# The multiply that makes LN2's shift moves from VectorE to GpSimd, and the planner's due times are set anew

## The chip, the cores and the metric

The kernel runs on one core of a Trainium2 chip. The time is the device time of one execution in microseconds; the kernel before took 4276.48 us, the median of three runs (4270.45 to 4277.21). The execution that was profiled has a span of 4280.8 us.

## The reference

One block of an image transformer, on 16 images of 128 channels x 96 x 96 pixels in float32:

```
xn1 = LN1(x)                         # over the 128 channels of a pixel
x   = x + attention(xn1)             # 8 heads, channel by channel: softmax of a 16 x 16 matrix per head
xn2 = LN2(x)                         # (x - mean) / sqrt(var + 1e-5) * w + b
h1  = w_in  x xn2                    # 128 -> 512 channels
h2  = depthwise 3x3 of h1            # nine taps for each of the 512 channels
x   = x + w_out x gelu(h2)           # 512 -> 128 channels
```

The change touches the step inside LN2 that makes, for every pixel, the numbers `rstd = (var + eps)^-0.5` and `nb = -mean * rstd`, with which the pixel's channels are scaled and shifted: `z = rstd * x + nb`.

## The kernel before

**Tiling.** An image has 24 units of 4 rows (384 pixels) and 8 bands of 12 rows (1152 pixels). The norms work on batches of 4 x 128 pixels; an image has 18, so LN1 has 288 batches in all and LN2 as many. For a batch, TensorE transposes the pixels to the partitions (`forth`, L572), VectorE takes two `bn_stats` (`stats`, L579), GpSimd makes `var/C + eps` (`variance`, L586) and raises it to -0.5 (`power`, L590). For LN2 VectorE then makes `nb` (`shift`, L594). ScalarE scales and shifts the transposed pixels (`scaled`, L621 for LN2, L617 for LN1), TensorE transposes back (`back`, L662), and ScalarE copies the result into the padded image (`place`, L666 and L668). In the first batches of the first image VectorE takes half of the scaling (L604 and L608).

**The feed-forward part.** The 512 hidden channels are four chunks of 128. For three of them, and in every second band for the fourth too, a conv job makes h1 with TensorE (`hidden`, L845), copies it to SBUF with ScalarE (`kept`, L850), and adds up nine taps: the first product is made by ScalarE (L861), two or three further products too, and those are added by accumulating DMAs that GpSimd issues (`add_products`, L869); the remaining five or six are multiply-adds of 128 x 1152 on VectorE (`tap`, L865). ScalarE ends the job with a gelu (L873). In the other bands the fourth chunk is nine matmuls per unit (L916) with a gelu of its own (L922). `ffn_out` multiplies by w_out (L939), and VectorE adds the result to x (L946). GpSimd also issues the accumulating DMAs that bring x in for LN2 (`add_x`, L542).

**What sets the order.** The program's order is written out by a planner (`Plan`) before anything runs. Each piece of work is put in with an engine, an assumed cost, and a due time: the place in the row of conv jobs, plus the offset that the table `AT` has for its kind. The planner plays the engines forward in time: an engine that is free takes, of the work whose inputs are there and whose buffers are free, the one with the earliest due time. The start times give one order, and the instructions are written in it. On the chip every engine then runs its own instructions strictly in that order, and semaphores hold an instruction until its inputs are there. So an instruction that waits holds up all that stands behind it on its engine. The tiles `st`, `ve`, `rstd` and `nb` come from a pool with four buffers for each (`small`), and the planner lets four batches be under way.

Of the kernel before, what the change touches and what calls it, by code (L numbers as in the profile page):

```python
# [9 lines left out]
F32 = mybir.dt.float32  # L10
AF = mybir.ActivationFunctionType
ALU = mybir.AluOpType
# [15 lines left out]
QT, QB = 4, 1  # L28
# [1 line left out]
X1_BUFS, XB_BUFS, PR_BUFS, H3_BUFS, ZT_BUFS = 2, 6, 5, 10, 3  # L30
IN_TURN = ("tr", "h3", "pr", "xb", "x1")
AT = dict(
    weights=5.95, zeros=1.3, load_a=-24.9, forth_a=-15.4, stats_a=-14.45, variance_a=-16.5, power_a=0.1,
    scaled_a=-8.2, gram=-10.45, back_a=-24.05, place_a=-20.25, attention=-20, mix=-9.75, residual=-0.2,
    mixed=-5.2, add_x=13.3, forth_b=-13.25, stats_b=-9.65, variance_b=-14, power_b=-10.85, shift_b=-26,
    scaled_b=4.45, back_b=-25.35, place_b=4.85, halo=7.55, hidden=0.1, kept=-2.95, product=-12.5,
    products=4.8, add_last=-15, tap=3.1, add_first=31.85, gelu=-8.35, conv=-0.05, conv_gelu=-13.5,
    out=4.05, add=-3.25, store=7.05,
)
STEP = dict(scaled=0.3, hidden=0.1, products=0.5, tap=0.166, conv=1.6, conv_tap=0.03, out=0.8, out_part=0.05)  # L40
SLACK = 300
# [4 lines left out]
T_VARIANCE = 420  # L46
# [4 lines left out]
class Plan:  # L51
# [14 lines left out]
    def op(self, engine, ns, place, work, reads, writes, result, own=None, dma=0, two=False):  # L66

        k = len(self.ops)
        needs = {}
        for t in reads:
            if t in self.writer:
                needs[self.writer[t]] = True
        for t in writes:
            if t in self.writer:
                needs[self.writer[t]] = True
            for r in self.readers.get(t, ()):  # L80
                needs[r] = True
        for t in reads:
            self.readers.setdefault(t, []).append(k)
        new = []
        for t in writes:
            self.writer[t], self.readers[t] = k, []
            if t[0] in self.free and t[:2] not in self.users and t[:2] not in new:
                new.append(t[:2])
        for t in {t[:2]: None for t in (*reads, *writes)}:
            if t[0] in self.free:  # L90
                self.users.setdefault(t, []).append(k)
                needs[self.users[t][0]] = True
        needs.pop(k, None)
        self.ops.append((engine, ns, place, work, list(needs), new, result, own or result, dma, two))
# [111 lines left out]
def tile_restormer_block(  # L206
# [24 lines left out]
    nc = tc.nc  # L231
    B, C, H, W = x.shape
    P = 128
# [61 lines left out]
    small = ctx.enter_context(tc.tile_pool(name="small", bufs=4))  # L295
# [43 lines left out]
    op = plan.op  # L339

    def at(kind, place):
        return place + AT[kind]
# [25 lines left out]
    def dve(ns, p, f, r, w, two=False):  # L368
        op("DVE", ns, p, f, r, w, ns + 120 + SLACK, ns + 120, two=two)
# [144 lines left out]
    def norm(i, second, place_of):  # L514

        name = f"{'b' if second else 'a'}{i}"
        ab = "_b" if second else "_a"
# [38 lines left out]
        def pixels(s, m):  # L556

            d = {}
# [15 lines left out]
            def stats(j):  # L574

                if j == 0:
                    d["st"] = small.tile([P, QB * QT // 2, 6], F32, tag="st", name=f"st_{name}_{m}")
                h, k = divmod(2 * j, QT)
                nc.vector.bn_stats(  # L579
                    d["st"][:, j, :], d["pT", qs[h]][:, k : k + 2, :].rearrange("p t c -> p c t")  # L580
                )
# [6 lines left out]
            def power():  # L588
                rstd = d["rstd"] = small.tile([P, QB * QT], F32, tag="rstd", name=f"rstd_{name}_{m}")
                nc.gpsimd.tensor_tensor(rstd, d["ve"], mhalf, ALU.pow)  # L590

            def shift():
                nb = d["nb"] = small.tile([P, QB * QT], F32, tag="nb", name=f"nb_{name}_{m}")
                nc.vector.scalar_tensor_tensor(nb, d["mv"][:, :, 1], -1.0, d["rstd"], ALU.mult, ALU.mult)  # L594

            def zT(q):
                zTs[q] = zT_bufs[plan.slot["zT", (name, q)]]
# [38 lines left out]
            trs, bt = [(key_, (name, q)) for q in qs], ("batch", (name, m))  # L636
# [2 lines left out]
                pe(110 * QT, at("forth" + ab, s), lambda q=q: forth(q), [xtok(u) for u in units], [tr])  # L639
            for j in range(QB * QT // 2):  # L640
                dve(341, at("stats" + ab, s), lambda j=j: stats(j), [trs[2 * j // QT]], [bt])
            op("POOL", T_VARIANCE, at("variance" + ab, s), variance, [], [bt], T_VARIANCE + 33 + SLACK)
            op("POOL", T_POWER, at("power" + ab, s), power, [], [bt], T_POWER + 33 + SLACK)
            if second:
                dve(80, at("shift" + ab, s), shift, [], [bt])
            for h, (q, tr) in enumerate(zip(qs, trs)):
                zt, sh = ("zT", (name, q)), s + STEP["scaled"] * h
                if by_dve:
# [45 lines left out]
        for m in range(NU * TPU // (QB * QT)):  # L694
            pixels(place_of(m * QB * QT), m)
            while u < NU and (u + 1) * TPU <= (m + 1) * QB * QT:
                channels(place_of(u * TPU), u)
                u += 1
# [325 lines left out]
```

## Time and profile before

| engine | busy us of 4280.8 | instructions |
|---|---|---|
| TensorE, matmul (PE) | 4201.1 | 17453 |
| VectorE (DVE) | 4141.5 | 4766 |
| ScalarE (ACT) | 4074.4 | 7278 |
| GpSimd (POOL) | 2423.4 | 2331 |

The profile's page names a group of equal instructions by line, engine, operation, and output<-input with buffer numbers left out, so `nb_b` is the tile `nb` of LN2 and `ve_a` the tile `ve` of LN1. After the first bar stand busy microseconds and the mean nanoseconds of one; after the second, the time for which the engine stood idle just before such instructions, and whom it waited for. An engine's busy time in stretches of the span shows three parts: a head of some 107 us (weights, the norms of the first image; VectorE is busy for 65.2 us of it), a body up to 4240 us in which the work of the images overlaps (VectorE is busy for 4045.9 of 4133.0 us), and a tail of 41 us. A matmul's end is modelled in this profile, so PE's busy time is more than what its work needs.

### The profile page before, as it was taken

What the parts mean: (1) busy time and instruction counts of PE and PEld (TensorE: products, weight loads), DVE (VectorE), ACT (ScalarE), POOL (GpSimd) and SP (SyncE); (2) the same over time, 40 slices, a digit from 0 to 9 for tenths busy, and PEclk for the clock granted to TensorE, in tenths of its full rate; (3) what the DMA queues carried; (4) which work ended last, traced back from release to release, by engine and by line L of the source; (5) the groups of instructions that cost most, each with busy time, mean ns of one, the idle gap of its engine ahead of it and who ended that gap; (6) DMA issues with size and microseconds to landing.
All of it is one profiled execution on the core that took longest, in us unless ns stands there. A gap on an engine that the chain in (4) does not pass through costs nothing.

```text
span 4280.8 us, 52546 instructions
## 1 busy us (share of the span) xinstructions
PE 4201.1 (98%) x17453; PEld 2677.0 (63%) x17453; DVE 4141.5 (97%) x4766; ACT 4074.4 (95%) x7278; POOL 2423.4 (57%) x2331
## 2 busy tenths in 40 slices
PE   8999999999999999999999999999999999999999
PEld 6566666666666666666666665666656666666555
DVE  6999999999999999999999999999999999999999
ACT  4999999999999999999999999999999999999996
POOL 4556556555556556656565665556656555555432
PEclk9999999999999999999999999999999999999999
DMA  2889899998998989989898998989889898998997
GB/s 86 181 181 202 184 200 196 191 199 187 194 195 191 193 186 209 194 186 204 178 194 185 192 200 179 198 186 202 184 181 201 187 198 190 191 194 168 187 187 162
DMA packets 197887, 802.87 MB, mean 188 GB/s; under 512 B 22896, under 2 KB 24304, under 8 KB 197616
## 3 DMA queue, kind: packets, MB, share of 16 engines
q0 software_dynamic: 158112, 647.70, 78.3%
q1 hardware_dynamic: 37152, 151.01, 9.7%
q8 instruction: 138, 2.26, 0.2%
q10 hardware_dynamic: 2352, 0.81, 0.1%
q14 instruction: 133, 1.09, 0.1%
HBM read 148.26 MB, written 75.50 MB: 52 GB/s over the span
## 4 chain that ended last, share of the span: by engine, by line
PE 55%; ACT 21%; DVE 14%; DMA 5%; issue 3%; POOL 2%; ACTq 0%; POOLq 0%; DVEq 0%
PE h L916 16%; PE h L939 13%; DVE h L865 12%; PE h L845 11%; ACT pr L861 5%; DMA h<-pr 3%; PE g L631 3%; PE h L530 3%; ACT h L850 3%; ACT h L861 2%; ACT zT L621 2%; ACT h L873 2%; PE pB_a L662 2%; PE pB_b L662 2%; ACT zT L617 2%
## 5 line engine op out<-in xcount | busy, mean ns | idle before, releaser
L865 DVE SCALAR_TENSOR_TENSOR h<-h,dw,h 128x1152 f32<-128x1152 f32 x2592 | 3554.6, 1409 | 17.3 <-ACT h L861 14.0
L861 ACT ACTIVATE pr<-h,dw 128x1152 f32<-128x1152 f32 x976 | 1307.9, 1357 | 9.7 <-DMA pr<-pr 9.4
L916 PE MATMUL h<-xn,comp 128*128 128x384 f32 x3564 | 1305.4, 487 | 5.0 <-ACT h L850 3.1
L939 PE MATMUL h<-h,woutT 128*128 128x384 f32 x3072 | 1158.5, 489 | 7.3 <-ACT h L850 3.4
L845 PE MATMUL h<-xn,winT 128*128 128x384 f32 (+1 forms) x2676 | 1043.3, 501 | 5.4 <-ACT h L850 2.7
L916 PEld LDWEIGHTS h<-xn,comp 128*128 128x128 f32 x3564 | 652.4, 190 | 420.6 <-ACT h L850 13.5
L869 POOL DMA_DIRECT2D pr<-pr x531 | 498.8, 939 | 680.8 <-ACT pr L861 478.2
L939 PEld LDWEIGHTS h<-h,woutT 128*128 128x128 f32 x3072 | 560.1, 190 | 356.6 <-issue 15.0
L850 ACT COPY h<-h 128x384 f32<-128x384 f32 (+1 forms) x1338 | 702.0, 590 | 34.1 <-PE h L845 25.0
L869 POOL DMA_DIRECT2D h<-pr x445 | 437.9, 993 | 503.5 <-DVE h L865 117.3
L845 PEld LDWEIGHTS h<-xn,winT 128*128 128x128 f32 x2676 | 484.4, 190 | 323.7 <-issue 53.1
L861 ACT ACTIVATE h<-h,dw 128x1152 f32<-128x1152 f32 x446 | 599.8, 1347 | 5.1 <-PE h L939 3.2
L873 ACT ACTIVATE h<-h 128x1152 f32<-128x1152 f32 x448 | 556.6, 1243 | 42.2 <-DMA h<-pr 39.9
L590 POOL TENSOR_TENSOR rstd_a<-ve_a,mhalf 128x4 f32<-128x4 f32 x288 | 520.0, 1806 | 11.4 <-POOL ve_a L586 0.2
L590 POOL TENSOR_TENSOR rstd_b<-ve_b,mhalf 128x4 f32<-128x4 f32 x288 | 492.8, 1715 | 10.3
L621 ACT ACTIVATE zT<-pT_b,nb_b,rstd_b 128x128 f32<-128x128 f32 x1132 | 452.4, 559 | 6.4 <-DVE nb_b L594 6.4
L586 POOL TENSOR_SCALAR ve_b<-st_b 128x4 f32<-128x4 f32 x288 | 286.4, 994 | 260.0 <-DVE st_b L579 254.2
L586 POOL TENSOR_SCALAR ve_a<-st_a 128x4 f32<-128x4 f32 x288 | 292.6, 1016 | 227.1 <-DVE st_a L579 223.0
L617 ACT ACTIVATE zT<-pT_a,rstd_a 128x128 f32<-128x128 f32 x1080 | 330.3, 461 | 23.6 <-POOL rstd_a L590 23.3
L631 PE MATMUL g<-zT 128*128 128x129 f32 x2304 | 307.4, 276 | 0.0
L530 PE MATMUL h<-xn,mwT 128*128 128x384 f32 x768 | 293.7, 490 | 5.8 <-ACT h L850 4.8
L631 PEld LDWEIGHTS g<-zT 128*128 128x128 f32 x2304 | 282.9, 193 | 1.5 <-ACT zT L617 0.5
(156 smaller groups left out, 3698.3 us busy)
## 6 DMA issues: line engine op xcount, KB each, us to landing
pr<-pr POOLq DMA_DIRECT2D x531, 576.0 KB, 6.2
h<-pr POOLq DMA_DIRECT2D x445, 576.0 KB, 6.9
x<-in_x_dram SPq DMA_DIRECT2D x128, 576.0 KB, 6.1
out_dram<-x SPq DMA_DIRECT2D x127, 576.0 KB, 4.7
x<-in_x_dram POOLq DMA_DIRECT2D x122, 576.0 KB, 7.2
out_dram<-x SPq DMA_DIRECT2D x3, 192.0 KB, 1.9
weights<-in_L_conv_w_in_dram ACTq DMA_DIRECT2D x1, 256.0 KB, 10.9
weights<-in_L_conv_w_out_dram ACTq DMA_DIRECT2D x1, 256.0 KB, 11.7
```

What stands on the lines that cost most here:

```text
L586: nc.gpsimd.tensor_scalar(ve, d["mv"][:, :, 2], 1.0 / C, EPS, ALU.mult, ALU.add)
L590: nc.gpsimd.tensor_tensor(rstd, d["ve"], mhalf, ALU.pow)
L621: nc.scalar.activation(zT(q)[:, k, :P], d["pT", q][:, k, :], AF.Identity, bias=d["nb"][:, t : t + 1], scale=d["rstd"][:, t : t + 1],)
L631: nc.tensor.matmul(grams[i][:, : P + 1], lhsT=zt[:, :P], rhs=zt, start=(q == 0 and k == 0), stop=(q == NU * TPU // QT - 1 and k == QT - 1),)
L845: nc.tensor.matmul(rows(ph), lhsT=winT[:, n, :], rhs=window(xn, r0 + r, e - r, 1), start=True, stop=True)
L850: nc.scalar.copy(window(h1_, r, e - r, 1), rows(d.pop(("ph", r))))
L861: nc.scalar.activation(to, shifted(t), AF.Copy, scale=dw[:, n, t : t + 1])
L865: nc.vector.scalar_tensor_tensor(h3, shifted(t), dw[:, n, t : t + 1], h3, ALU.mult, ALU.add)
L869: nc.gpsimd.dma_start(out=to, in_=d["pr", t], accum_op=ALU.add)
L873: nc.scalar.activation(h3, h3, AF.Gelu)
L916: nc.tensor.matmul(d["pc"], lhsT=comp[:, t, :], rhs=window(xn, r0 + dy, UR, dx), start=(t == 0), stop=(t == 8),)
L939: nc.tensor.matmul(rows(d["po"]), lhsT=woutT[:, n, :], rhs=h3s[g, n][:, s * UR : (s + 1) * UR, :], start=(k == 0), stop=(k == NCH - 1),)
```

## The change

`shift` is split. VectorE makes `nb = -mean` from the statistics alone (`less`), which needs no result of GpSimd. GpSimd then multiplies `nb` by `rstd` in place, behind `power`. In the planner `less` is put in behind `stats` with a key of its own, and `shift` behind `power`, with the assumed cost of `variance` (420 ns). The form of the instruction on VectorE changes from `scalar_tensor_tensor` (mean, rstd) to `tensor_scalar` (mean). All offsets of `AT` but a few are new, so the order of the whole program is planned anew; the instructions themselves are the same but for these.

```
 AT = dict(
-    weights=5.95, zeros=1.3, load_a=-24.9, forth_a=-15.4, stats_a=-14.45, variance_a=-16.5, power_a=0.1,
-    scaled_a=-8.2, gram=-10.45, back_a=-24.05, place_a=-20.25, attention=-20, mix=-9.75, residual=-0.2,
-    mixed=-5.2, add_x=13.3, forth_b=-13.25, stats_b=-9.65, variance_b=-14, power_b=-10.85, shift_b=-26,
-    scaled_b=4.45, back_b=-25.35, place_b=4.85, halo=7.55, hidden=0.1, kept=-2.95, product=-12.5,
-    products=4.8, add_last=-15, tap=3.1, add_first=31.85, gelu=-8.35, conv=-0.05, conv_gelu=-13.5,
-    out=4.05, add=-3.25, store=7.05,
+    weights=8.1, zeros=2.6, load_a=-26, forth_a=-15.4, stats_a=-15.1, variance_a=-16.5, power_a=-1.8,
+    scaled_a=-9.35, gram=-10, back_a=-25.05, place_a=-22.25, attention=-20.55, mix=-10.3, residual=-1.25,
+    mixed=-5.15, add_x=14.65, forth_b=-13.8, stats_b=-11.25, variance_b=-15.4, power_b=-11.85,
+    less_b=-17.75, shift_b=-26.4, scaled_b=2.15, back_b=-26.6, place_b=3.2, halo=6.95, hidden=0.55,
+    kept=-5.3, product=-13.45, products=4.05, add_last=-15.55, tap=6.15, add_first=32.9, gelu=-9.35,
+    conv=0.5, conv_gelu=-14.25, out=4.5, add=-1.4, store=6.1,
 )
...
+            def less():
+                nb = d["nb"] = small.tile([P, QB * QT], F32, tag="nb", name=f"nb_{name}_{m}")
+                nc.vector.tensor_scalar(nb, d["st"].rearrange("p j (t v) -> p (j t) v", v=3)[:, :, 1], -1.0, None, ALU.mult)
+
             def shift():
-                nb = d["nb"] = small.tile([P, QB * QT], F32, tag="nb", name=f"nb_{name}_{m}")
-                nc.vector.scalar_tensor_tensor(nb, d["mv"][:, :, 1], -1.0, d["rstd"], ALU.mult, ALU.mult)
+                nc.gpsimd.tensor_tensor(d["nb"], d["nb"], d["rstd"], ALU.mult)
...
+            if second:
+                dve(80, at("less_b", s), less, [bt], [("less", (name, m))])
             op("POOL", T_VARIANCE, at("variance" + ab, s), variance, [], [bt], T_VARIANCE + 33 + SLACK)
             op("POOL", T_POWER, at("power" + ab, s), power, [], [bt], T_POWER + 33 + SLACK)
             if second:
-                dve(80, at("shift" + ab, s), shift, [], [bt])
+                op("POOL", T_VARIANCE, at("shift" + ab, s), shift, [("less", (name, m))], [bt], T_VARIANCE + 33 + SLACK)
```

## The prediction

> **What bounds the kernel now.** I read the page's busy times first, then its costliest groups.
>
> ```profile
> PE 4201.1 (98%) x17453; PEld 2677.0 (63%) x17453; DVE 4141.5 (97%) x4766; ACT 4074.4 (95%) x7278; POOL 2423.4 (57%) x2331
> L865 DVE SCALAR_TENSOR_TENSOR h<-h,dw,h 128x1152 f32<-128x1152 f32 x2592 | 3554.6, 1409 | 17.3 <-ACT h L861 14.0
> L590 POOL TENSOR_TENSOR rstd_b<-ve_b,mhalf 128x4 f32<-128x4 f32 x288 | 492.8, 1715 | 10.3
> L586 POOL TENSOR_SCALAR ve_b<-st_b 128x4 f32<-128x4 f32 x288 | 286.4, 994 | 260.0 <-DVE st_b L579 254.2
> ```
>
> Three engines are near full at once. Of VectorE's idle time (4280.8 - 4141.5 = 139.3 us), 41.8 us lie in the head and 10.4 in the tail; 87.1 us lie in the body. So VectorE is the fullest real engine there (PE's ends are modelled), and what is to be had is what makes it wait. The list of waits of VectorE says what that is, with total, number and longest:
>
> ```profile
> DVE nb_b L594 <- POOL rstd_b L590: 28.1, 28, 2.1
> DVE st_a L579 <- PE pT_a L572: 18.4, 20, 2.8
> DVE x L946 <- PE h L939: 15.6, 27, 1.6
> DVE h L865 <- ACT h L861: 14.0, 12, 3.3
> ```
>
> The instruction that the change takes off its wait is the largest single wait of VectorE, a third of the idle time in its body. It is late in 28 of 288 batches, 1.0 us each. Whether that reaches the end is told by the chain of waits, read stretch by stretch (start, length, what):
>
> ```profile
> 2136.24 0.88 POOL pr L869
> 2137.12 0.87 POOL ve_a L586
> 2137.99 2.19 POOL rstd_b L590
> 2140.18 0.02 issue
> 2140.20 0.16 DVE nb_b L594
> 2140.37 1.34 DVE h L865
> ```
>
> A late DMA issue and LN1's variance push LN2's power back, `nb` waits for it, and the taps behind wait too. In the whole chain `POOL rstd_b` stands in 15 pieces, 21.2 us together; 13 of them end in `nb_b`. The chain is mostly PE (55%), ACT (21%) and DVE (14%), POOL 2%: those waits are links of a chain that changes engine often.
>
> **What the Trainium skill says.** *SBUF — State Buffer*, "Who interferes with whom": a VectorE instruction with two SBUF inputs contends with a GpSimd instruction that reads SBUF, and the one that came second waits. The trace agrees on GpSimd's side: `variance` takes 0.184 us at the least and 1.272 us in the median, the spread of a running tap's rest; the longest `power` took 10.97 us. It shows no cost on the other side: 2592 taps took 1389 to 1468 ns. *Perfetto Trace Analysis*, "Identifying Dependency Chains": an instruction that waits for several engines may get separate wait instructions ahead of it; the trace has 216 of them ahead of VectorE's adds at L946, 21 ns the shortest. *VectorE: DVE Perf Modes*, "The DRAIN you can't avoid": a semaphore between VectorE instructions costs nothing extra. The trace differs a little: dependent VectorE instructions in a row (L799) stand idle for 0.6 us over 16, 35 ns each.
>
> **The change part by part.**
>
> (1) `nb` on VectorE no longer waits for `power`. 28.1 us of idle time go from L594; the gain lies between 0 and 28.1. The 13 chain pieces at 28.1/28 = 1.0 us are 13 us on the chain. The other 15 waits are not on it, but VectorE is the fullest engine: I take a third, 5 us. Value: -18.
>
> (2) `less` in place of `shift` on VectorE: 288 x 157 ns go, and 288 of a tensor_scalar with few columns come, nearest row `n` at L774, 128x2, 154 ns: -0.9 us, and as much either way. It waits for its own `stats`; in the listing of the new order it stands directly behind the second one in 3 of 288 batches, at some 35 ns each. Value 0.
>
> (3) `shift` on GpSimd: 288 instructions of 128x4. No row is a plain multiply there; below stands the shortest `variance`, 0.18 us, above the mean `power`, 1.72. I take the mean `variance`, 0.994, as it has the same reads and waits: 286 us more, 2423 to 2710, 63% of the span. What hides it is GpSimd's idle time, 1857 us. Yet its queue is in order. Behind a `shift` stand LN1's `variance` and `power` and the DMA issues of L869 and L542; `shift` itself waits for `power` just ahead and for a `less` long done. In the listing it follows its `power` at once in 98 batches and with one instruction between in 190. Who waits behind GpSimd is ScalarE: gelu for the added products 39.9 us, LN1's scaling for `rstd_a` 23.3, products for a free buffer 9.4, together 72.6. If these grow as GpSimd's work (286/2423 = 12%), ScalarE waits for 8.6 us more, and I count half for the end: +4. LN2's own scaling waited 6.4 us for `nb`; between its last input and its first use stand 4.7 taps' worth of VectorE work in the median before and 5.3 after (5% below 1.2 and 1.7), so this wait should stay small: 0. Ends: 0 and, if all 72.6 us double, +29 (at 0.4, roughly what lies between ACT's share of the chain and one half).
>
> (4) New waits on VectorE. Statistics now have GpSimd as last reader (before, `shift` on VectorE itself came later), so `stats` must wait for the `variance` of four batches ago. Instructions of VectorE that name GpSimd in a wait go from 336 to 560, separate wait instructions from 327 to 782 on VectorE and 819 to 958 on ScalarE. That `variance` is long done; what remains is (455 + 139) x 21 ns = 12.5 us if none were hidden behind a running tap of 1.4 us. Value +1, ends 0 and 12.5.
>
> (5) The new order. No engine gets other work: 2592 taps, the same matmuls, activations and loads; the loads and stores of SP move by at most one place against each other. In taps of VectorE, the distance from the issue of the last addition to its gelu goes from 5.6 to 5.8 in the mean, from gelu to the first matmul that reads it from 12.8 to 11.6, from the last product to its addition from 1.4 to 1.2. These speak for neither sign. VectorE's other idle time in the body is 59 us; I let the order give or take a quarter, 15 us. Value 0.
>
> Sum: -18 + 0 + 4 + 1 + 0 = -13, so 4280.8 - 13 = 4267.8 of span. The median of the runs is 4.3 us below the profiled span; that gives **4263.5 us**.
>
> **The rivals.**
>
> *Full gain.* All 28.1 us go, and a good order takes 10 more from other waits, against +5 from (3) and (4): -33, 4243.5 us. For it: VectorE has 98% in the body, so nearly every wait of it counts. Against: PE's and ScalarE's waits (gelu for DMA 39.9, `kept` for PE 25.0) lie elsewhere and stay.
>
> *The wait is absorbed.* VectorE gets to its next meeting 1 us earlier and waits there, or ScalarE at L621 waits for GpSimd's product instead: so the change does not do what it says. Then (1) gives 5 and (3), (4) take 5: 4276.5 us. For it: PE holds 55% of the chain. Against: VectorE has few other waits, about one in 46 us.
>
> *Slower: GpSimd's queue becomes the limit.* Each `shift` waits for a tap's end (variance's median 1.27 us) and pushes the DMA issues behind it. If ScalarE's waits behind GpSimd double, (3) is +29; with only the 13 chain microseconds won and +1 from (4), +17: 4293.5 us. It decides once ScalarE waits over 45 us more behind GpSimd (18/0.4), beyond 118 in all. For it: one `power` was held for 10.97 us, and GpSimd already waits for late inputs, so lateness adds up. Against: 43% of GpSimd is idle.
>
> **How the numbers follow.** The measurement can tell some 0.2% from no change, 8.6 us: faster is below 4267.9, slower above 4285.1. Forecast (4254 to 4269) 0.42, full gain 0.16, absorbed 0.22, slower 0.20. From these: faster 0.57, as a sliver of the forecast's lies above the line, same 0.23, slower 0.20. The unknown order and (4) widen each case; 4240 leaves out half of the full gain's cases, 4290 half of the slower ones. Range 4240 to 4290.
>
> **What would show it.** (1): no idle time before L594, and VectorE's idle time in the body near 70 us. (2): `less` at 150 to 160 ns. (3): `shift` near 1 us, GpSimd near 2710 us, ScalarE's waits behind it 75 to 90 us. (4): idle time before `stats` with GpSimd as releaser below 2 us. It is wrong if VectorE's idle time keeps its 139 us with other names, or if gelu's wait for its DMA passes 60 us.

## The result, and the profile after

The changed kernel takes 4298.8 us, the median of four runs (4295.65 to 4315.9), against 4276.84 us before: ratio 1.0063, 95% interval 1.0041 to 1.0086. In a second session it stood at 1.0058 (1.0037 to 1.0078). So it is slower by 0.6%, 22 us in the first session and 24 in the second; forecast was 0.3% faster. Ratios are to the kernel before in the same session, with a 95% interval in brackets; a "point" is one per cent of that time, some 43 us.

The page of the kernel after, busy times and the groups that answer to those shown of before:

```profile
PE 4206.6 (98%) x17453; PEld 2682.5 (62%) x17453; DVE 4147.2 (97%) x4766; ACT 4077.1 (95%) x7278; POOL 2579.1 (60%) x2619
L870 DVE SCALAR_TENSOR_TENSOR h<-h,dw,h 128x1152 f32<-128x1152 f32 x2592 | 3559.8, 1411 | 16.4 <-ACT h L866 12.6
L590 POOL TENSOR_TENSOR rstd_b<-ve_b,mhalf 128x4 f32<-128x4 f32 x288 | 524.0, 1820 | 10.5
L586 POOL TENSOR_SCALAR ve_b<-st_b 128x4 f32<-128x4 f32 x288 | 278.7, 972 | 123.0 <-DVE st_b L579 122.1
```

Work grew little: GpSimd by 155.7 us, which it can hide, VectorE by 5.7 us. From the longer list of groups come the two instructions into which `shift` was split:

```profile
L597 POOL TENSOR_TENSOR nb_b<-nb_b,rstd_b 128x4 f32<-128x4 f32 x288 | 250.6, 871 | 7.7
L594 DVE TENSOR_SCALAR nb_b<-st_b 128x4 f32<-128x4 f32 x288 | 49.8, 173 | 0.2
```

The wait at L594 is gone (28.1 to 0.2 us), as meant. But VectorE's idle time rose, from 139.3 to 4295.3 - 4147.2 = 148.1 us. Its list of waits says where:

```profile
DVE st_b L579 <- PE pT_b L572: 23.3, 36, 3.4
DVE st_a L579 <- PE pT_a L572: 23.0, 30, 3.3
DVE x L951 <- PE h L944: 16.5, 23, 3.8
DVE h L870 <- ACT h L866: 12.6, 13, 3.3
DVE x L951 <- ACT h L855: 11.0, 1, 11.0
```

VectorE now waits for TensorE's transposes (the two statistics rows: 5.3 + 18.4 us before, 46.3 after). And one wait, in the last line, is 11.0 us long by itself. The timeline around it, those lines of it that matter, in order of start (start, length, engine, work, idle time before and releaser):

```profile
3963.57 12.04 DVE L870 SCALAR_TENSOR_TENSOR h<-h,dw,h 128x1152 f32<-128x1152 f32 x9
3965.80 10.71 POOL L590 TENSOR_TENSOR rstd_b<-ve_b,mhalf 128x4 f32<-128x4 f32 x1
3976.59 0.20 POOL L597 TENSOR_TENSOR nb_b<-nb_b,rstd_b 128x4 f32<-128x4 f32 x1
3976.82 1.50 ACT L624 ACTIVATE zT<-pT_b,nb_b,rstd_b 128x128 f32<-128x128 f32 x4 [9.36 <-POOL nb_b L597]
3979.80 1.65 PE L530 MATMUL h<-xn,mwT 128*128 128x384 f32 x2 [9.08 <-ACT h L855]
```

Ten taps run back to back from 3962.24 to 3975.61 us (the view, cut at 3964, shows nine). GpSimd's power, begun under the third, isn't done until 0.9 us after the row's end: 10.71 us for work that took 1.0 us at the least. Below, this is called the hold. ScalarE stands in front of the scaling that needs it for 9.36 us, TensorE behind ScalarE for 9.08, and VectorE, its row done, for 11.0. The chain of waits goes straight through it:

```profile
3965.80 10.71 POOL rstd_b L590
...
3976.59 0.21 POOL nb_b L597
3976.80 0.03 issue
3976.82 1.50 ACT zT L624 x4
```

In the kernel before no LN2 power took over 3.65 us, though LN1's, which has no reader on VectorE, did (up to 10.97). That suggested a reading which the prediction hadn't: the wait at L594 was also a **stop** of VectorE, and in a stop the power is let in. It is tested as theory C below.

### The profile page after: what moved, and what is told of

Its sections match the earlier page's. It is cut to its first block, busy times and chain, and to the rows that moved or that the text cites. A ratio compares the mean times of both kernels' runs of the same rounds, so it can differ in the third digit from the quotient of the medians.

```text
span 4295.3 us, 53570 instructions
## 1 busy us (share of the span) xinstructions
PE 4206.6 (98%) x17453; PEld 2682.5 (62%) x17453; DVE 4147.2 (97%) x4766; ACT 4077.1 (95%) x7278; POOL 2579.1 (60%) x2619
## 4 chain that ended last, share of the span: by engine, by line
PE 55%; ACT 26%; DVE 8%; DMA 4%; issue 4%; POOL 3%; ACTq 0%; POOLq 0%; DVEq 0%
PE h L921 16%; PE h L944 13%; PE h L850 11%; ACT pr L866 7%; DVE h L870 6%; ACT h L855 4%; PE g L634 3%; DMA h<-pr 3%; ACT h L866 3%; ACT h L878 3%; PE h L530 3%; ACT zT L624 3%; ACT zT L620 2%; PE pT_b L572 2%; PE pB_a L667 2%
## 5 line engine op out<-in xcount | busy, mean ns | idle before, releaser
L866 ACT ACTIVATE pr<-h,dw 128x1152 f32<-128x1152 f32 x976 | 1323.7, 1376 | 7.3 <-DMA pr<-pr 7.3
L944 PE MATMUL h<-h,woutT 128*128 128x384 f32 x3072 | 1145.4, 488 | 6.0 <-ACT h L855 3.3
L855 ACT COPY h<-h 128x384 f32<-128x384 f32 (+1 forms) x1338 | 715.0, 595 | 37.7 <-PE h L850 29.8
L874 POOL DMA_DIRECT2D h<-pr x445 | 450.6, 1038 | 473.4 <-DVE h L870 76.9
L878 ACT ACTIVATE h<-h 128x1152 f32<-128x1152 f32 x448 | 560.6, 1252 | 49.6 <-DMA h<-pr 47.8
L590 POOL TENSOR_TENSOR rstd_b<-ve_b,mhalf 128x4 f32<-128x4 f32 x288 | 524.0, 1820 | 10.5
L590 POOL TENSOR_TENSOR rstd_a<-ve_a,mhalf 128x4 f32<-128x4 f32 x288 | 509.9, 1774 | 9.3 <-POOL ve_a L586 0.2
L624 ACT ACTIVATE zT<-pT_b,nb_b,rstd_b 128x128 f32<-128x128 f32 x1132 | 451.5, 558 | 11.1 <-POOL nb_b L597 11.1
L586 POOL TENSOR_SCALAR ve_a<-st_a 128x4 f32<-128x4 f32 x288 | 266.9, 927 | 229.6 <-DVE st_a L579 217.2
L620 ACT ACTIVATE zT<-pT_a,rstd_a 128x128 f32<-128x128 f32 x1080 | 335.7, 482 | 19.5 <-POOL rstd_a L590 19.2
```

The lines of the kernel that those rows point to most:

```text
L586: nc.gpsimd.tensor_scalar(ve, d["mv"][:, :, 2], 1.0 / C, EPS, ALU.mult, ALU.add)
L624: nc.scalar.activation(zT(q)[:, k, :P], d["pT", q][:, k, :], AF.Identity, bias=d["nb"][:, t : t + 1], scale=d["rstd"][:, t : t + 1],)
L855: nc.scalar.copy(window(h1_, r, e - r, 1), rows(d.pop(("ph", r))))
L866: nc.scalar.activation(to, shifted(t), AF.Copy, scale=dw[:, n, t : t + 1])
L874: nc.gpsimd.dma_start(out=to, in_=d["pr", t], accum_op=ALU.add)
L878: nc.scalar.activation(h3, h3, AF.Gelu)
```

## The experiments

Three theories. **A**: the new offsets make the loss. **B**: GpSimd's multiply makes it, by what it delays. **C**: VectorE's lost stop makes it. Edits are on the changed kernel ("after") or on the one before.

**1. The split with the old offsets** (after, `AT` of before with `less_b=-16.15`).

> The split of the shift as in the changed kernel, but planned with the old offsets (and 6.5 for less ahead of stats, as in the changed kernel). Theory A, the new offsets make the loss: 4260 to 4278 us, as VectorE's 28 us of waits go. Theory B, GpSimd's multiply makes the loss, as it delays what is queued behind it: 4290 us or more. Theory C, VectorE no longer stops for the power, so that back-to-back taps keep GpSimd's power out for longer: 4285 to 4300 us, and the longest LN2 power over 5 us, against 3.6 us before.

Measured: 4318.9 us, 1.0111 (1.0098 to 1.0125). A falls as the whole cause: without the new offsets the split is worse still. The number lies where B put it (4290 us or more) and above C's range. But the split planned with the old offsets gives a third order, which differs from both kernels', so the run doesn't decide between B and C. Its longest LN2 power took 5.0 us and one multiply 6.8 us. Between 1520 and 1600 us of its span TensorE is busy for 72.0 of 80 us; what the order does badly there wasn't followed up.

**2. The new offsets alone** (before, `AT` of after).

> The new offsets alone; shift stays on VectorE behind the power. Theory A (offsets): 4290 to 4305 us, with VectorE waiting for the power for some 30 us as before. Theory B (multiply): 4270 to 4282 us. Theory C (VectorE's lost stop): 4270 to 4282 us, and no LN2 power over 5 us.

Measured: 4281.6 us, 1.0025 (1.0016 to 1.0035). The new order costs 0.25 points, some 11 us, by itself. No GpSimd power was long: 3.5 us at most.

**3. The new order without the multiply.**

```
             def shift():
-                nc.gpsimd.tensor_tensor(d["nb"], d["nb"], d["rstd"], ALU.mult)
+                pass
```

> The changed kernel in its own order on every engine, with GpSimd's multiply left out (so LN2 subtracts the bare mean): 288 GpSimd instructions of 0.87 us fewer. Theory A: 4293 to 4300 us, as before this edit. Theory B: 4270 to 4282 us. Theory C: 4290 to 4300 us, as the power has no reader on VectorE here either; LN2 powers over 5 us stay.

Measured: 4291.3 us, 1.0041 (1.0026 to 1.0055). Without any multiply the middle of the interval keeps about two thirds of the loss, and the long hold stays: the power of the same batch took 11.20 us. That speaks against B as the main cause in this order; numbers 5 and 9 price the multiplies more closely.

**4. A spare multiply in the old order** (before, all other instructions in place).

```
                 nc.gpsimd.tensor_tensor(rstd, d["ve"], mhalf, ALU.pow)
+                if second:
+                    spare = small.tile([P, QB * QT], F32, tag="spare", name=f"spare_{name}_{m}")
+                    nc.gpsimd.tensor_tensor(spare, d["ve"], rstd, ALU.mult)
```

> The kernel before in its own order on every engine, with a spare GpSimd multiply of 128x4 behind each LN2 power, read by no one. Theory A: 4276 to 4282 us. Theory B: 4290 to 4300 us. Theory C: 4276 to 4282 us.

Measured: 4298.9 us, 1.0069 (1.0057 to 1.0081). Here B is right: in an order that wasn't planned for it, a multiply costs 29/288 = 0.1 us of the end each time, and no power was held for more than 3.5 us.

**5. One multiply of 288 back on VectorE** (after): a stop, put three taps behind that batch's `less`.

```
             def shift():
-                nc.gpsimd.tensor_tensor(d["nb"], d["nb"], d["rstd"], ALU.mult)
+                engine = nc.vector if (i, m) == (15, 1) else nc.gpsimd
+                engine.tensor_tensor(d["nb"], d["nb"], d["rstd"], ALU.mult)
```

> The changed kernel with one of its 288 multiplies put back on VectorE, at the same place of the written order: that of batch 1 of image 15, whose power GpSimd held for 10.7 us under a row of taps. Theory C (a stop of VectorE lets the power in): that power takes 2 to 3 us, ScalarE's wait of 9.4 us and VectorE's of 11.0 us at that place go, and the ratio to the kernel before falls from 1.0063 by about 9/4277 = 0.2 points, to 1.004. Theory B (the multiplies): nothing but one multiply of 0.9 us changes, 1.006.

Measured: 4282.0 us, 1.0025 (1.0017 to 1.0033). The middle of the interval is 14 us below number 10's, more than half of the loss, for one instruction; the interval lies below both of the changed kernel's. The timeline at that batch:

```profile
3958.04 1.41 POOL L590 TENSOR_TENSOR rstd_b<-ve_b,mhalf 128x4 f32<-128x4 f32 x1
3959.49 0.16 DVE L598 TENSOR_TENSOR nb_b<-nb_b,rstd_b 128x4 f32<-128x4 f32 x1 [0.93 <-POOL rstd_b L590]
3959.57 6.73 DVE L871 SCALAR_TENSOR_TENSOR h<-h,dw,h 128x1152 f32<-128x1152 f32 x5
```

VectorE stops for 0.93 us, the power takes 1.41 instead of 10.71, and the row of taps goes on behind. A stop of 0.9 us saves a wait of 11.0. So the hold makes this part of the loss, and a stop ends it.

But C's word "lost" doesn't fit: this batch had no stop to lose. In number 2, where VectorE still made `nb`, the same batch shows no idle time before `nb` (no bracket in the last line):

```profile
3954.62 1.77 POOL L590 TENSOR_TENSOR rstd_b<-ve_b,mhalf 128x4 f32<-128x4 f32 x1
3955.49 2.73 DVE L865 SCALAR_TENSOR_TENSOR h<-h,dw,h 128x1152 f32<-128x1152 f32 x2
3958.15 0.15 DVE L594 SCALAR_TENSOR_TENSOR nb_b<-st_b,rstd_b 128x4 f32<-128x4 f32 x1
```

In the kernel before it shows none either. What the change took away is VectorE's reader of the power. In its order VectorE can't pass that reader before the power has ended, so a hold lasts no longer than the taps in front of it. The profiles fit this bound: where VectorE read every LN2 power (before, 2, 4, 6, 7, 11), the longest took 3.51 to 3.66 us; in the other eight, which read none or a single one, 3.60 to 11.20, and 4.9 or more in all but number 12. That the batch would have been held in the order of number 2 without its reader wasn't tried.

**6 and 7. What of the multiply costs** (before, a spare instruction at the place of number 4): `memset(spare, 1.0)`, which reads nothing, and `tensor_tensor(spare, d["ve"], d["ve"], ALU.mult)`, which doesn't wait for the power.

> The kernel before in its own order, with a spare GpSimd memset of 128x4 behind each LN2 power: an instruction that reads nothing and waits for nothing. If it is the slot in GpSimd's queue that costs (theory B1): 4285 us or more beside 4270. If it is the wait for the power's end or for the end of a tap that costs (B2, B3): 4268 to 4275 us.

> The kernel before in its own order, with a spare GpSimd multiply of 128x4 that reads the variance and not the power: it contends with the taps, but doesn't wait for the power's end. B2, the wait for the power's end, which keeps the DMA issue behind it from starting while the power runs: 4268 to 4278 us. B3, the wait for the end of a tap: 4290 to 4300 us, as the multiply that read the power.

Measured: 1.0009 (1.0000 to 1.0018) and 1.0045 (1.0027 to 1.0062). The slot in the queue costs next to nothing, and an instruction that reads costs most of what number 4 cost; waiting for the power's end too may add to it (1.0069, but the intervals overlap a little). The same place in the groups of number 6, then of number 7:

```profile
L593 POOL MEMSET spare_b<- 128x4 f32 x288 | 62.2, 216 | 0.0
```

```profile
L593 POOL TENSOR_TENSOR spare_b<-ve_b 128x4 f32<-128x4 f32 x288 | 221.7, 770 | 0.0
```

The mean is 0.216 against 0.770 us. The multiply's shortest took 0.187 us, so most of its time is waiting; that it waits for a tap to end is the likely reading. What this delays shows in gelu's wait for its added products: 39.9 us before, 42.1 with the memset, 57.4 and 61.2 with the multiplies of 7 and 4.

**8. No shift at all** (before). The mean over the channels is taken out of `winT` and `comp` once, at the start; `shift` goes, and LN2 is scaled like LN1.

```
+        def no_mean(t, gives):
...
+                nc.tensor.matmul(d["pc"], lhsT=v["centre"], rhs=t, start=True, stop=True)
...
+        no_mean(winT.rearrange("p n c -> p (n c)"), "in")
...
-            if second:
-                dve(80, at("shift" + ab, s), shift, [], [bt])
```

> The kernel before without any shift: the mean over the channels is taken out of the weights (w_in and its nine depthwise products, centred once at the start, as LN1's weights are), which is exact where LN2's bias has no mean over the channels, as here, where it is zero. No nb, no wait for it, and ScalarE scales LN2 as it does LN1 (0.46 in place of 0.56 us, 1132 times). Old offsets, but a new order follows, as the planner counts less for ScalarE. If waits of VectorE and ScalarE's work count for the end: 4200 to 4250 us. If all of it is absorbed in other waits: 4265 to 4280 us.

Measured: 4243.5 us, 0.9933 (0.9913 to 0.9953), faster than both kernels. ScalarE's scaling of LN2:

```profile
L620 ACT ACTIVATE zT<-pT_b,rstd_b 128x128 f32<-128x128 f32 x1132 | 342.5, 450 | 5.5 <-POOL rstd_b L604 5.5
```

From 559 to 450 ns, 1132 times, are 123 us of work off ScalarE. VectorE's `nb` and its wait are gone as well, and the order is planned anew; all together brought some 29 us at the end, and the parts weren't separated. It holds where LN2's bias has no mean over the channels.

**9. The new order with neither multiplies nor the long hold** (after: `shift` does nothing but the one VectorE multiply of number 5).

> The changed kernel without GpSimd's multiplies, but with the one on VectorE (batch 1 of image 15): LN2 subtracts the bare mean in all other batches. It holds the order of the new offsets with neither the waits of VectorE, nor the multiplies, nor the long hold. Beside the new offsets with the old shift (1.0025) it prices VectorE's 41 us of waits: if they count in full, ratio 0.993; if half, 0.998; if they are absorbed, 1.002. Beside the same with the multiplies (1.0025) it prices those: 0.1 to 0.3 points lower.

Measured: 4278.5 us, 1.0025 (1.0017 to 1.0033). That is number 5 without 287 multiplies: they cost nothing that can be told in the order planned for them, against the 0.1 to 0.3 points expected. And it stands where number 2 stands, with the same offsets but without VectorE's 41.0 us of waits: those were worth nothing that can be told either. In both comparisons the two intervals leave room for some 5 us. The waits of VectorE in number 2, then in number 9:

```profile
DVE nb_b L594 <- POOL rstd_b L590: 41.0, 42, 2.9
DVE st_a L579 <- PE pT_a L572: 12.2, 16, 2.4
DVE st_b L579 <- PE pT_b L572: 11.2, 24, 1.4
DVE x L946 <- PE h L939: 8.3, 13, 2.0
```

```profile
DVE st_a L579 <- PE pT_a L572: 20.8, 27, 2.9
DVE st_b L579 <- PE pT_b L572: 19.7, 29, 2.9
DVE x L952 <- PE h L945: 17.1, 25, 3.8
```

The first line goes, and the others grow by 25.9 us. VectorE's whole idle time goes from 139.0 to 133.0 us (span less busy time), and its work grew by 4.8: the waits moved to other names, as they would if VectorE arrives earlier and waits there.

**10. The changed kernel again**, in the session of 9 and 11.

> The changed kernel as it is, beside the same runs of the kernel before as the other three. Both theories: 1.005 to 1.007, some 0.3 points above the one with a single multiply on VectorE; 1.003 or less would say that the gain of that single instruction was a difference of sessions.

Measured: 4291.7 us, 1.0058 (1.0037 to 1.0078). That power took 10.71 us again. Against number 9 it is 13.3 us slower.

The changed kernel and numbers 3, 5, 9 and 10 write their 2592 taps in one order, so the starts of the taps in their profiles can be laid side by side. At the tap under which the power begins, the changed kernel is 6.6 us behind number 9, number 10 is 1.6 behind and number 3 is 1.5. From the first tap after the hold to the last they are 16.6, 11.2 and 10.9 us behind, without change. So the hold moves the end by 10.0, 9.6 and 9.4 us. Number 5 is 1.2 us ahead of number 9 on both sides of it. What remains of the 13 or 14 us between the medians isn't tied to this place.

**11. Three stops for LN1** (before: `nc.vector.tensor_copy(stop, rstd)` behind three of LN1's powers).

> The kernel before with three VectorE copies of 128x4 that read rstd of LN1 directly behind the power, in the three batches whose power was held for 7.7 to 11.0 us (batch 2 of image 11, 8 of 12, 2 of 13). Theory C: those three powers take 1 to 3 us, ScalarE's 11.6 us and VectorE's 6.6 us of waits there go against three stops of 1 to 2 us; ratio 0.997 to 0.999. If a stop of VectorE doesn't let the power in: the powers stay at 7 us or more, 1.000 to 1.001.

Measured: 4277.2 us, 1.0018 (1.0009 to 1.0027). A miss of the forecast (0.997 to 0.999), though the stops did what C says. The power held for 10.97 us was let in:

```profile
2997.47 1.67 POOL L590 TENSOR_TENSOR rstd_a<-ve_a,mhalf 128x4 f32<-128x4 f32 x1
2999.18 0.17 DVE L593 COPY stop_a<-rstd_a 128x4 f32<-128x4 f32 x1 [0.93 <-POOL rstd_a L590]
2999.26 9.38 DVE L868 SCALAR_TENSOR_TENSOR h<-h,dw,h 128x1152 f32<-128x1152 f32 x7
```

The other two took 2.12 and 2.41 us, and the waits of ScalarE (11.6 us) and VectorE (6.6) there are gone. Yet the whole isn't faster. These holds had cost VectorE 2.8, 2.8 and 1.0 us of waits, not 11. Why the total came out 0.18 points above stays open.

**12. No shift, new offsets** (number 8 with `AT` of after).

> The kernel without any shift (mean taken out of the weights), planned with the new offsets in place of the old. If the new offsets are the worse ones by themselves (as they were with the shift on VectorE, 1.0025): 0.995 to 0.997, against 0.993 with the old. If they suit an order without VectorE's wait: 0.990 to 0.993.

Measured: 4249.2 us, 0.9952 (0.9935 to 0.9970). No better than the old offsets, rather worse, though the intervals overlap.

## Why the prediction was wrong, step by step

**Step (1) failed: it took VectorE's wait for a loss, at -18 us.** In the new order its removal is worth nothing that can be told (number 9 against 2, both 1.0025, to some 5 us); in the old order no run separates it. The prediction counted idle time per piece of the chain as time of the end. With three engines at 95% and more, other waits of VectorE grew by 25.9 us where that one went. The "absorbed" rival said so and got 0.22. The count was off too: in the chain `nb` follows ten of the 15 pieces, not 13, which would have given -16; that isn't what failed.

**Step (3) failed in its last term: LN2's scaling, waiting for `nb`, was put at 0.** Of the 11.1 us that ScalarE waited there, 9.36 are the one hold, and it moved the end by 9.4 to 10.0 us. The prediction argued from how much VectorE work lies between input and use in the median and at 5%; what happened is one batch of 288. It also quoted the power of 10.97 us without asking why it was LN1's and never LN2's.

The rest of (3) stayed within its ends: +4 was forecast, and 287 multiplies cost nothing measurable (5 against 9). In the order before they cost 19 to 29 us (7 and 4). That the planner's due times hide them in the new order isn't shown: number 1, planned with the multiply in it as well, was the slowest of all. ScalarE's three waits behind GpSimd went from 72.6 to 47.8 + 19.2 + 7.3 = 74.3 us, not 81. So the "slower" rival came nearest with its 4293.5 us by luck: its mechanism, these waits growing past 118 us, didn't occur.

**Step (5), the order, was within its ends**: 0 forecast, +11 us measured (1.0025, numbers 2 and 9), of the 15 allowed. Why the new order is slower stays open.

**Step (2)** was off by a little: `less` took 173 ns in the mean, not 157, 4.6 us of work in all. **Step (4)** held: statistics waited for GpSimd for 0.5 us.

Together: 11 us for the order and some 10 for the hold are 21, against 22 and 24 measured; the rest is within the intervals. The prediction's own signs show it: idle time before L594 gone, as said; VectorE's idle time in the body not near 70 us but 95.9 (4133.0 - 4037.1); and over the whole span not below 139 us but 148.1, with other names, which it had named as the sign of being wrong.

## What to carry to other kernels

Where three engines are nearly full, an engine's largest wait isn't yet a gain: look for the wait that takes its place, and price the removal by an experiment that leaves the order alone. Before a wait is taken away, ask what it bounds: here the instruction that waited also kept a row of taps from passing a late power, and without it one hold cost some 10 us, which a pause of 0.9 us would have saved. If neither engine can take a small step for nothing, look for a way to do without the step, as the mean in the weights did.

## What the runs showed of the hardware that wasn't expected

- A row of VectorE multiply-adds with two SBUF inputs can keep a small GpSimd operation from ending for many instructions in a row, not only to the end of the running one: 8 taps, 10.71 us. Most are let in sooner (the median LN2 power of the changed kernel took 1.97 us); what makes a row closed wasn't found.
- Such holds repeat. In the new order the same batch was held for 10.71 us in both profiles of the changed kernel and for 11.20 in number 3; in the old order LN1's three for 8.77, 10.97 and 7.75 us, and with the memset for 8.78, 10.61 and 7.75. They hang on the timing: with a spare multiply in the old order (4 and 7) no LN1 power took over 3.5 and 4.0 us.
